# A round of its own for T1, its low parts on VectorE, a later bias add and a first pair worked two chunks at a time

## The chip, the cores and the metric

The kernel runs on one core of a Trainium2 chip. A core has TensorE (PE, matrix products into PSUM), ScalarE (ACT), VectorE (DVE) and GpSimd (POOL) for elementwise work, and SyncE (SP), which here only issues transfers; transfers are also issued from POOL's queue, and could be from ACT's. Each engine works its own queue in order, and engines wait for each other by semaphores. The metric is the device time of one execution in microseconds (us). The kernel before takes 494.98 us, the median of three runs (494.9 to 495.29).

## The reference, cut to what matters

The input x is 64 x 64 x 1024 float32 (B, C, T). Each batch element picks one of 16 matrices of 64 x 64; a gated low-rank feed-forward layer follows, and x is added back.

```python
y = einsum('bct,bcd->bdt', x, weights[condition])     # mixes the 64 channels of one b
logits = einsum('bsd,ed->bse', y, gate_w)             # 8 experts
w, sel = top_k(logits, 2); w = softmax(w)             # w_full: 8 weights, 6 of them zero
result = einsum('bsd,od->bso', y, base_w) + base_b
low = einsum('bsd,erd->ebsr', y, lora_A)              # 8 experts x rank 16
result += 2.0 * einsum('ebsr,eor,bse->bso', low, lora_B, w_full)
out = x + result
```

## The kernel before, in words

**Tiles.** The 4096 tokens (b, c) are 32 tiles of 128. For a tile i, the product z of x with all weights is formed first: lora_A (128 columns), gate (8) and base_w (1024), 1160 columns in all, in four chunks c = 0 to 3 of 344, 236, 344, 236 columns. The channel mixing comes afterwards, as a product of z with a 128 x 128 block matrix gathered for the tile (`bdr`), since it acts on tokens alone. Float32 accuracy comes from splitting each operand in a high part (a rounded copy in `fp32r`) and a low part (the rest), and from three matmuls high x high, high x low, low x high (`zstep`, line 306). A split is two steps: a copy on ACT that rounds (`copy`, line 202), and a subtraction on DVE (`sub`, line 199, two inputs in SBUF). The tiles are `xh`/`xl` for x, `wh`/`wl` for weights, `zh`/`zl` for z, `bdh`/`bdl` for the gathered matrix.

**Plain tiles and pairs.** The inner dimension (8 blocks of 128, index k) is cut in halves h of four blocks, the columns in halves n of 580. So the weights are four blocks B11, B12, B21, B22, each of 4 x 128 rows and 344 + 236 columns (s = 0, 1). The first four tiles (two pairs) are plain: z = x1 B1n + x2 B2n. The other 28 tiles go by pairs, by Strassen's method in its seven-product form: products p1 (B11), p2 (B21), q3 (B22), and p6, p7, q4, q5 with the weight sums T2, T3, T4, T1, where T1 = B11 + B12, T3 = B12 + B22, T2 = B11 + T3, T4 = B21 + T2. The order in the first such pair is p1, p2, q3, p6, p7, q4, q5 (`FIRST`), with `post` work of other chunks between them; p2 is accumulated onto p1 in p1's banks, once p1 has been copied out. B12 is used by plain tiles alone, and its place in SBUF (`BLOCK`) is that of T4: T4 is written over B12 when the plain tiles are done with it.

**Weights.** `load_w` brings a piece of two k blocks and one s (344 or 236 KB) into one of the staging buffers `st`; `split_w` splits it into `wh`/`wl`. For the plain tiles, 16 pieces go round staging buffers 0 to 3. For the sums, `sum_w(s, k)`, called four times, loads the four pieces of all blocks again into `st` 0 to 3, forms the four sums there (`plus`, line 259, two inputs in SBUF) and splits all four; the low part goes to DVE or POOL, as the planner finds. `st[4]` is the place into which the first Strassen pair copies p1 (`u`); its other partial results are in `st` 1 to 3.

**After a chunk.** `post` mixes: for c = 0, three matmuls (line 337) into bank a0 or a1, then `gate` (the router, on DVE and ACT, lines 363 to 378), a transpose of the scaled `low` on PE (`tr`, line 383) and its split `lth`/`ltl`; for c > 0, the low-rank products and the mixing together into bank o0 or o1. `finish` (line 344) adds the result to `xtok`, which holds the rows of x plus bias, and `store` writes a tile. For the first four tiles the bias is added on DVE or POOL (line 277) as soon as the rows have landed, ahead of all `finish` steps of the tile; for later ones a transfer with accumulation does it.

**What sets the order.** All steps are put in a list (`add`, with an engine, a cost, what they read and write), and `Program.run` plays a list schedule on those costs: a step's `due` time gives each earlier step the latest time at which it may start (`late`), and an idle engine takes the ready step with the smallest. `ORDER` gives the due times of the plain matmuls, `pr.horizon` those of other steps. Loads without inputs are held back until ten microseconds before their `late` (`early`). The instructions are issued in that order, so each engine's queue is fixed when the program is built, by estimated times. SP issues all loads of weights and x, POOL the gathers, the stores and the bias transfers.

**The start.** `ORDER` has chunk 0 of tiles 0 and 1 together, block by block, then chunk 1 of tile 0, chunk 1 of tile 1 and so on. 29 small matmuls on zeroed data run first (line 193).

Of the kernel before, what the change touches and what calls it, by code (L numbers as in the profile page):

```python
# [20 lines left out]
P = 128  # L21
# [35 lines left out]
class Program:  # L57
# [7 lines left out]
    def add(self, engine, cost, fn, reads=(), writes=(), due=None, first=False, lag=0.0, early=False):  # L65


        n = len(self.steps)
        engine, cost = (e if isinstance(e, (list, tuple)) else [e] for e in (engine, cost))
        deps = set()  # L70
        for b in list(reads) + list(writes):
            if b in self.writer:
                deps.add(self.writer[b])
        for b in writes:
            deps.update(self.readers.get(b, ()))
        for b in reads:
            self.readers.setdefault(b, []).append(n)
        for b in writes:
            self.writer[b], self.readers[b] = n, []
        deps.discard(n)  # L80
        self.steps.append(dict(eng=dict(zip(engine, cost)), fn=fn, deps=deps, first=first, lag=lag,
                               due=self.horizon if due is None else due,
                               early=early or (SP in engine and not reads)))

    def run(self):
        steps, n = self.steps, len(self.steps)
        succ = [[] for _ in steps]
        for i, s in enumerate(steps):
            for d in s["deps"]:
                succ[d].append(i)  # L90
        hop = lambda a, b: SAME[a] if a == b else HOP[a]
        late = [0.0] * n
        for i in reversed(range(n)):
            s = steps[i]
            c, e = min(s["eng"].values()), next(iter(s["eng"]))
            late[i] = min([s["due"] - c] + [late[j] - hop(e, next(iter(steps[j]["eng"]))) - s["lag"] - c
                                            for j in succ[i]])
        left = [len(s["deps"]) for s in steps]
        ready, end, by = [0.0] * n, [0.0] * n, [None] * n
        free = dict(START)  # L100
        cand = {e: set() for e in HOP}

        def offer(i):
            for e in steps[i]["eng"]:
                t = max([0.0] + [end[d] + hop(by[d], e) + steps[d]["lag"]
                                 for d in steps[i]["deps"]])
                if steps[i]["early"]:
                    t = max(t, late[i] - AHEAD)
                t += MARGIN if steps[i]["first"] else 0.0
                cand[e].add((i, t))  # L110

        for i in range(n):
            if not left[i]:
                offer(i)
        done = 0
        while done < n:
            best = None
            for e, c in cand.items():
                if c:
                    t = max(free[e], min(r for _, r in c))  # L120
                    if best is None or t < best[0]:
                        best = (t, e)
            t, e = best
            i, r = min(((i, r) for i, r in cand[e] if r <= t + 1e-9),
                       key=lambda q: (not steps[q[0]]["first"], late[q[0]], q[0]))
            for f in steps[i]["eng"]:
                cand[f] = {q for q in cand[f] if q[0] != i}
            end[i], by[i] = t + steps[i]["eng"][e], e
            free[e] = end[i]
            steps[i]["fn"](e)  # L130
            done += 1
            for j in succ[i]:
                left[j] -= 1
                if not left[j]:
                    offer(j)
        return max(end)
# [3 lines left out]
def cond_ffn_kernel(ctx, tc, xT, x, idx, cw, wall, bias, lb, out):  # L140
# [15 lines left out]
    def many(n, shape, dt, name):  # L156
# [6 lines left out]
    BLOCK = (("b11", "t4"), ("b21", "b22"))  # L163
# [3 lines left out]
    NXR, NXA, NZ = 6, 4, 3  # L167
    xr, xtok = many(NXR, [P, KH, P], F32, "xr"), many(3, [P, T], F32, "xtok")
    xh, xl = many(NXA, [P, KH, P], F32R, "xh"), many(NXA, [P, KH, P], F32R, "xl")
    st = many(5, [P, 2 * CS[0]], F32, "st")  # L170
# [6 lines left out]
        ("mx", 8), ("l2", 14), ("d", E), ("e", E), ("wf", E), ("s", 1), ("r", 1))}  # L177
# [7 lines left out]
    warm = sb.tile([P, 8], F32, name="warm")  # L185
    nc.vector.memset(warm, 0.0)
    nc.scalar.activation(warm, warm, AF.Exp)
# [34 lines left out]
    def split_x(r, pieces=1, hi=ACT, lo=DVE):  # L222

        j, n = take("xa", NXA), KH // pieces
        for k in range(0, KH, n):
# [4 lines left out]
                [("xr", r, b) for b in q] + [("xh", j, b) for b in q], [("xl", j, b) for b in q])  # L230
        return j

    def sum_x(o, a, b, f):
        keys = lambda r: [("xr", r, q) for q in range(KH)]
        add(DVE, tt_cost(P * KH), lambda e: nc.vector.tensor_tensor(xr[o], xr[a], xr[b], f),  # L235
            [k for r in (a, b) if r != o for k in keys(r)], keys(o))
# [4 lines left out]

    def load_w(j, h, n, s, k):
        add(SP, DMA * 8 * P * CS[s], lambda e: nc.sync.dma_start(piece(j, s), wall[h][n][s][:, k:k + 2, :]),
            writes=[("st", j, 0), ("st", j, 1)])

    def split_w(j, m, s, k, hi=ACT, lo=DVE):
# [4 lines left out]
        lo = lo if isinstance(lo, tuple) else (lo,)  # L251
        add(lo, [tt_cost(n, e) for e in lo], lambda e: sub(e, wl[m, s][:, a], piece(j, s), wh[m, s][:, a]),
            src + [("wh", m, s, b) for b in q], [("wl", m, s, b) for b in q])

    def sum_w(s, k):
        keys = lambda j: [("st", j, 0), ("st", j, 1)]

        def plus(o, a, b):
            add(DVE, tt_cost(2 * CS[s]), lambda e: nc.vector.tensor_tensor(piece(o, s), piece(a, s), piece(b, s), ALU.add),  # L259
                [q for j in (a, b) if j != o for q in keys(j)], keys(o))  # L260
        for j, (h, n) in enumerate(((0, 0), (0, 1), (1, 1), (1, 0))):
            load_w(j, h, n, s, k)
        plus(0, 0, 1)
        plus(1, 1, 2)
        plus(2, 2, 0)
        plus(3, 3, 2)
        for j, m in ((2, "t2"), (1, "t3"), (3, "t4"), (0, "t1")):
            split_w(j, m, s, k, lo=(DVE, POOL))

    def load_tok(i):  # L270
# [5 lines left out]
        if early:  # L276
            add((DVE, POOL), (1.22, tt_cost(T, POOL)), lambda e: eng[e].tensor_tensor(xtok[j], xtok[j], bias_bc, ALU.add),  # L277
                ["bias"], keys)
        else:
            add(POOL, 1.1, lambda e: nc.gpsimd.dma_start(xtok[j], bias.broadcast_to([P, T]), accum_op=ALU.add),  # L280
                writes=keys, lag=5.0)

    def load_cond(i):
# [7 lines left out]
        add(DVE, 0.25, lambda e: sub(e, bdl[j], bdr[j], bdh[j]), [("bdr", j), ("bdh", j)], [("bdl", j)])  # L291
# [63 lines left out]
    def gate(i, b):  # L355
# [9 lines left out]
        def op(o, a, f, eng=DVE, cost=0.17):  # L365
            add(eng, cost, lambda e: f(), [(b, i % 2) for b in a], [(b, i % 2) for b in o])

        ts, stt = nc.vector.tensor_scalar, nc.vector.scalar_tensor_tensor
        op(["mx"], ["low"], lambda: nc.vector.max(v["mx"], lg14))
        op(["d"], ["mx", "low"], lambda: ts(v["d"], lg, v["mx"][:, 6:7], None, ALU.subtract), cost=0.2)  # L370
        op(["e"], ["d"], lambda: nc.scalar.activation(v["e"], v["d"], AF.Exp), ACT, 0.2)
        op(["l2"], ["mx", "low"], lambda: nc.vector.match_replace(v["l2"], v["mx"], lg14, LOWEST), cost=0.25)
        op(["wf", "s"], ["l2", "e"], lambda: stt(v["wf"], v["l2"][:, :E], LOWEST, v["e"], ALU.is_equal, ALU.mult,  # L373
                                                 accum_out=v["s"]), cost=0.3)
# [3 lines left out]
            v["wf"].unsqueeze(2).broadcast_to([P, E, R]), ALU.mult, ALU.mult), cost=0.3)  # L378
# [32 lines left out]
    ORDER = [(i, 0, k) for k in range(KT) for i in range(2)]  # L411
    ORDER += [(i, c, k) for i, c in ((0, 1), (1, 1), (0, 2), (0, 3), (1, 2), (1, 3)) for k in range(KT)]
# [28 lines left out]

    def load_split_w(h, n, s, k, **engines):
        j = stage[0] % 4
        stage[0] += 1
# [7 lines left out]
    def first_loads():  # L452
        for h in range(2):
            for i in range(2):
                load_split_x(i, h, lo=DVE)
                load_split_w(h, 0, 0, 2 * i)
# [12 lines left out]
    for h in range(2):  # L469
        for k in range(0, KH, 2):  # L470
            load_split_w(h, 0, 1, k)
    load_cond(0)
    load_cond(1)
    for s in range(2):
        for h in range(2):
            for k in range(0, KH, 2):
# [8 lines left out]
                                                          ALU.subtract), lraw + ["lbh"], ["lbl"])  # L485
# [8 lines left out]
    zb = [f"z{take('z', 4)}" for _ in range(2)]  # L494
    for k in range(KT):
        for i in range(2):
            plain(i, 0, (k,), zb[i])
    for i in range(2):
        post(i, 0, split_z(CS[0], bank[zb[i]][:, :CS[0]], zb[i]))
    for i, c in ((0, 1), (1, 1), (0, 2), (0, 3), (1, 2), (1, 3)):  # L500
        b, n = f"z{take('z', 4)}", CS[c % 2]
        plain(i, c, range(KT), b)
        post(i, c, split_z(n, bank[b][:, :n], b))
        if c == 3:
            store(i, range(4))
    for q in range(1, NPLAIN):
        pr.horizon = ends[q] + LAG
        for i in (2 * q, 2 * q + 1):
# [4 lines left out]
            for c in range(4):  # L513
                b, n = f"z{take('z', 4)}", CS[c % 2]
                plain(i, c, range(KT), b)
                post(i, c, split_z(n, bank[b][:, :n], b))
            store(i, range(4))
    for s in range(2):
        for k in range(0, KH, 2):
            pr.horizon = ends[0] + (2 * s + k / 2 + 1) / 4 * (ends[NPLAIN - 1] - ends[0])  # L520
            sum_w(s, k)

# [41 lines left out]
    def pair(q):  # L564
        a, b = 2 * q, 2 * q + 1
        bx, by = (("z0", "z1"), ("z2", "z3"))[::1 if q % 2 else -1]
        u, v, w = 4 if q == NPLAIN else q % 2, 2, 3
# [3 lines left out]
        def combine(o, x, y, f, bs, reads=()):  # L571

            def then(s):
                at = {"o": part(o, s), "u": part(u, s), "v": part(v, s), "t": part(1, s), "z": z(bs, s)}
# [14 lines left out]
        if q == NPLAIN:  # L589

            t = 1
# [87 lines left out]
```

## Time and profile before

| | |
|---|---|
| median of three runs | 494.98 us (494.9 to 495.29) |
| the profiled execution's own time | 495.26 us |
| its span, first to last instruction | 493.5 us |
| PE busy | 480.2 us, 97% |
| DVE busy | 340.5 us, 69% |
| ACT busy | 173.2 us, 35% |
| POOL busy | 96.6 us, 20% |
| granted TensorE clock, mean | 0.993 |
| moved by transfers | 78.28 MB, 159 GB/s |
| loads of weights | 16 of 344 KB, 16 of 236 KB |

Times in the profile count from the start of the span. A line names the source line, the engine, the operation, what it writes and reads, and how often it ran. An arrow in "idle before" or in the list of waits names what ended the wait. The clock is a share of full speed. A busy time of matmuls is not throughput: they are pipelined, and the distance between starts tells their pace.

### The profile page before, as it was taken

The page shows a single profiled execution, that of the slowest core. Times are in us where ns is not written, and L with a number is a line of the kernel's source. Part 1 is how long each engine was busy: PE and PEld are TensorE (multiplying, and loading weights), DVE is VectorE, ACT ScalarE, POOL GpSimd, SP SyncE. Part 2 cuts the span into 40 slices and gives each one's busy share as a digit, 9 for nine tenths or more (in the row PEclk, how much of TensorE's full clock was granted, in tenths as well). Part 3 has the DMA queues.
Part 4 walks back from the last instruction along what each step waited for, and adds up shares of the span by engine and source line. Part 5 has one row for each costly group of instructions (what it writes and reads, how often), then busy time and mean ns, then how long its engine had stood idle before and what let it go on. Part 6 is the DMA issues. An engine that isn't in the chain of part 4 may idle for free.

```text
span 493.5 us, 9361 instructions
## 1 busy us (share of the span) xinstructions
PE 480.2 (97%) x3565; PEld 477.3 (97%) x3565; DVE 340.5 (69%) x930; ACT 173.2 (35%) x429; POOL 96.6 (20%) x110
## 2 busy tenths in 40 slices
PE   7999799899999999999999999999999999999996
PEld 6999799799999999999999999999999999999996
DVE  5768776885767666676667768666675686667664
ACT  6643324342332324233232433323232242323331
POOL 3015324411112030210203021030302103032010
PEclk8999999999999999999999999999999999999999
DMA  8793724942828275381835728192561727447162
GB/s 269 220 351 121 241 89 124 295 92 106 214 62 254 60 201 153 110 219 30 266 82 176 177 81 237 36 283 69 176 178 55 234 66 247 107 162 200 43 168 90
DMA packets 29325, 78.28 MB, mean 159 GB/s; under 512 B 3665, under 2 KB 7137, under 8 KB 29281
## 3 DMA queue, kind: packets, MB, share of 16 engines
q1 hardware_dynamic: 19872, 45.16, 27.7%
q0 software_dynamic: 9408, 32.53, 25.9%
q8 instruction: 28, 0.46, 0.4%
q14 instruction: 17, 0.13, 0.1%
HBM read 60.90 MB, written 16.78 MB: 157 GB/s over the span
## 4 chain that ended last, share of the span: by engine, by line
PE 85%; DMA 7%; DVE 4%; issue 1%; POOL 1%; ACT 1%; SPq 0%; DVEq 0%; POOLq 0%
PE ps_z L306 66%; PE ps_o L337 14%; DMA st<-in_w 6%; PE ps_a L337 5%; DVE st L259 2%; DMA xr<-in_xT 1%; POOL wl_t L199 1%; PE ps_a L383 1%; DVE xtok L344 1%; DVE wl_t L199 0%; DVE xl L199 0%; ACT wh_b L202 0%; DVE wf L373 0%; DVE zl L199 0%; DVE xtok L277 0%
## 5 line engine op out<-in xcount | busy, mean ns | idle before, releaser
L306 PE MATMUL ps_z<-wh_t,xh 128*128 128x344 f32 x480 | 143.7, 299 | 1.7 <-DVE st L576 1.3
L306 PE MATMUL ps_z<-wl_t,xh 128*128 128x344 f32 x480 | 142.6, 297 | 0.6 <-POOL wl_t L199 0.6
L306 PE MATMUL ps_z<-wh_t,xl 128*128 128x344 f32 x480 | 142.7, 297 | 0.0
L306 PE MATMUL ps_z<-wh_b,xh 128*128 128x344 f32 (+1 forms) x432 | 131.3, 304 | 2.0 <-ACT wh_b L202 1.4
L306 PE MATMUL ps_z<-wh_b,xl 128*128 128x344 f32 (+1 forms) x432 | 129.8, 300 | 0.4 <-DVE wl_b L199 0.4
L306 PE MATMUL ps_z<-wl_b,xh 128*128 128x344 f32 (+1 forms) x432 | 129.8, 300 | 0.2 <-DVE wl_b L199 0.2
L202 ACT CAST xh<-xr 128x512 fp32r<-128x512 f32 (+1 forms) x110 | 66.1, 605 | 83.6 <-PE ps_z L306 59.7
L199 DVE TENSOR_TENSOR xl<-xr,xh 128x512 fp32r<-128x512 f32 (+1 forms) x110 | 74.0, 677 | 28.0 <-ACT xh L202 26.2
L306 PEld LDWEIGHTS ps_z<-wh_t,xh 128*128 128x128 f32 x480 | 90.9, 189 | 2.3 <-DVE st L576 1.5
L306 PEld LDWEIGHTS ps_z<-wl_t,xh 128*128 128x128 f32 x480 | 91.0, 189 | 0.8 <-POOL wl_t L199 0.8
L306 PEld LDWEIGHTS ps_z<-wh_t,xl 128*128 128x128 f32 x480 | 90.8, 189 | 0.0
L306 PEld LDWEIGHTS ps_z<-wh_b,xh 128*128 128x128 f32 x432 | 83.0, 192 | 2.8 <-ACT wh_b L202 1.7
L306 PEld LDWEIGHTS ps_z<-wh_b,xl 128*128 128x128 f32 x432 | 82.8, 192 | 0.8 <-DVE wl_b L199 0.6
L306 PEld LDWEIGHTS ps_z<-wl_b,xh 128*128 128x128 f32 x432 | 82.9, 192 | 0.4 <-DVE wl_b L199 0.4
L344 DVE TENSOR_TENSOR xtok<-ps_o,xtok 128x344 f32<-128x344 f32 (+1 forms) x96 | 41.9, 438 | 33.5 <-PE ps_o L337 32.3
L202 ACT CAST zh<-st 128x344 fp32r<-128x344 f32 (+1 forms) x84 | 36.5, 436 | 72.6 <-PE ps_o L337 33.9
L351 POOL DMA_DIRECT2D out<-xtok x30 | 17.5, 585 | 209.8 <-DVE xtok L344 209.5
L576 DVE TENSOR_TENSOR st<-st,ps_z 128x344 f32<-128x344 f32 x84 | 38.0, 452 | 14.9 <-PE ps_z L306 14.9
L280 POOL DMA_DIRECT2D xtok<-in_bias x28 | 25.7, 917 | 109.0 <-DMA xtok<-in_x 107.7
L202 ACT CAST zh<-ps_z 128x344 fp32r<-128x344 f32 (+1 forms) x44 | 17.5, 401 | 72.7 <-PE ps_z L306 55.6
L235 DVE TENSOR_TENSOR xr<-xr,xr 128x512 f32<-128x512 f32 x56 | 38.5, 687 | 0.6
L199 DVE TENSOR_TENSOR zl<-st,zh 128x344 fp32r<-128x344 f32 (+1 forms) x84 | 37.9, 451 | 1.2 <-ACT zh L202 1.1
(71 smaller groups left out, 668.9 us busy)
## 6 DMA issues: line engine op xcount, KB each, us to landing
xtok<-in_x SPq DMA_DIRECT2D x32, 512.0 KB
xr<-in_xT SPq DMA_DIRECT2D x60, 256.0 KB
out<-xtok POOLq DMA_DIRECT2D x30, 512.0 KB, 5.3
xtok<-in_bias POOLq DMA_DIRECT2D x28, 512.0 KB, 5.3
st<-in_w SPq DMA_DIRECT2D x16, 344.0 KB
st<-in_w SPq DMA_DIRECT2D x16, 236.0 KB
xr<-in_xT SPq DMA_DIRECT2D x8, 128.0 KB
bdr<-in_cw,rows POOLq DMA_INDIRECT x32, 5.0
```

Of the source, the lines that this page charges most:

```text
L199: eng[e].tensor_tensor(o, a, b.bitcast(F32), ALU.subtract)
L202: (nc.scalar.copy if e == ACT else nc.vector.tensor_copy)(o, a)
L235: add(DVE, tt_cost(P * KH), lambda e: nc.vector.tensor_tensor(xr[o], xr[a], xr[b], f), [k for r in (a, b) if r != o for k in keys(r)], key ...
L259: add(DVE, tt_cost(2 * CS[s]), lambda e: nc.vector.tensor_tensor(piece(o, s), piece(a, s), piece(b, s), ALU.add), [q for j in (a, b) if j ...
L280: add(POOL, 1.1, lambda e: nc.gpsimd.dma_start(xtok[j], bias.broadcast_to([P, T]), accum_op=ALU.add), writes=keys, lag=5.0)
L306: nc.tensor.matmul(z, l[a][:, ka, :], w[m, s][:, ka, :], start=(start and q == 0), stop=(stop and q == 2), skip_group_check=True)
L337: nc.tensor.matmul(d, l, r, start=(start and m == 0), stop=(stop and m == len(mms) - 1), skip_group_check=True)
L344: add(DVE, 0.09 + 0.00104 * (s.stop - s.start), lambda e: nc.vector.tensor_tensor(xtok[j][:, o], bank[b][:, s], xtok[j][:, o], ALU.add), [ ...
L351: add(POOL, 1.0, lambda e: nc.gpsimd.dma_start(out[i * P:(i + 1) * P, o], xtok[j][:, o]), src, lag=2.0)
L383: add(PE, 0.107, lambda e: nc.tensor.matmul(tp, low[i % 2][:, :ER], ident, is_transpose=True, start=False, stop=False, skip_group_check=True),
L576: add(DVE, 0.09 + 0.00104 * CS[s], lambda e: nc.vector.tensor_tensor(at["o"], at[x], at[y], f), [bs[s]] + [("st", j, s) for j in reads if ...
```

## The change

1. **B12 and T1.** B12 takes the place of T1 in SBUF, no longer that of T4. `sum_w` forms and splits T3, T2 and T4 from the four loaded pieces. T1 has rounds of its own behind them (`sum_w1`, four calls), each of which loads B11's and B12's pieces anew, adds and splits them.
2. **Staging.** All weight pieces go round five staging buffers. The loads of weights are no longer held back. The first Strassen pair keeps its partial results in `st` 0, 4, 1, 2 (u, v, w, t), and its first products are in banks z0 and z1.
3. **DVE alone.** The low parts of T1 to T4 and the bias add of the plain tiles go to DVE only. The planner gets a flag (`port`) on DVE steps with two inputs in SBUF, such that two of these don't run at once in its plan.
4. **Bias.** For the first four tiles it is added behind the last `finish` of the tile, ahead of the store.
5. **The first pair.** Chunks 0 and 1 of tiles 0 and 1 are worked together, two k blocks at a time; the loads of weights for chunk 1 come in between. Then chunk 2 of both tiles and chunk 3 of both.
6. **The first piece of weights** is issued from ACT's queue, ahead of ACT's table load.
7. **The router.** The largest logit is negated on ACT and given to the exponential as its bias, in place of a subtraction on DVE, for all 32 tiles.

```diff
-    def add(..., lag=0.0, early=False):
+    def add(..., lag=0.0, early=None, port=False):
...
-                    t = max(free[e], min(r for _, r in c))
+                    t = max(free[e], min(max(r, port) if steps[i]["port"] else r for i, r in c))
...
+            if steps[i]["port"]:
+                port = end[i]
...
-    BLOCK = (("b11", "t4"), ("b21", "b22"))
+    BLOCK = (("b11", "t1"), ("b21", "b22"))
...
-    NXR, NXA, NZ = 6, 4, 3
+    NXR, NXA, NZ, NST = 6, 4, 3, 5
...
+    nc.scalar.dma_start(piece(0, 0), wall[0][0][0][:, 0:2, :])
+    begun = [True]
+    warm = sb.tile([P, 8], F32, name="warm")
+    nc.vector.memset(warm, 0.0)
+    nc.scalar.activation(warm, warm, AF.Exp)
...
     def load_w(j, h, n, s, k):
-        add(SP, DMA * 8 * P * CS[s], lambda e: nc.sync.dma_start(piece(j, s), wall[h][n][s][:, k:k + 2, :]),
-            writes=[("st", j, 0), ("st", j, 1)])
+        add(SP, DMA * 8 * P * CS[s], lambda e, begun=begun.pop() if begun else False: None if begun else
+            nc.sync.dma_start(piece(j, s), wall[h][n][s][:, k:k + 2, :]),
+            writes=[("st", j, 0), ("st", j, 1)], early=False)
...
     def sum_w(s, k):
...
-        plus(0, 0, 1)
-        plus(1, 1, 2)
-        plus(2, 2, 0)
-        plus(3, 3, 2)
-        for j, m in ((2, "t2"), (1, "t3"), (3, "t4"), (0, "t1")):
-            split_w(j, m, s, k, lo=(DVE, POOL))
+        b12, b22, b11, b21 = js = [next_stage() for _ in range(4)]
+        for j, (h, n) in zip(js, ((0, 1), (1, 1), (0, 0), (1, 0))):
             load_w(j, h, n, s, k)
+        for o, b, m in ((b12, b22, "t3"), (b11, b12, "t2"), (b21, b11, "t4")):
+            plus_w(o, o, b, s)
+            split_w(o, m, s, k)
+
+    def sum_w1(s, k, j):
+        for q in range(2):
+            load_w(j + q, 0, q, s, k)
+        plus_w(j, j, j + 1, s)
+        split_w(j, "t1", s, k)
...
-        if early:
-            add((DVE, POOL), (1.22, tt_cost(T, POOL)), lambda e: eng[e].tensor_tensor(xtok[j], xtok[j], bias_bc, ALU.add),
-                ["bias"], keys)
-        else:
+        if not early:
...
+    def late_bias(i):
+        j = i % 3
+        add(DVE, 1.22, lambda e: nc.vector.tensor_tensor(xtok[j], xtok[j], bias_bc, ALU.add), ["bias"],
+            [("xtok", j, c) for c in range(4)], port=True)
...
-        op(["d"], ["mx", "low"], lambda: ts(v["d"], lg, v["mx"][:, 6:7], None, ALU.subtract), cost=0.2)
-        op(["e"], ["d"], lambda: nc.scalar.activation(v["e"], v["d"], AF.Exp), ACT, 0.2)
+        op(["nm"], ["mx"], lambda: nc.scalar.mul(v["nm"], v["mx"][:, 6:7], -1.0), ACT, 0.2)
+        op(["e"], ["nm", "low"], lambda: nc.scalar.activation(v["e"], lg, AF.Exp, bias=v["nm"]), ACT, 0.2)
...
-    ORDER = [(i, 0, k) for k in range(KT) for i in range(2)]
-    ORDER += [(i, c, k) for i, c in ((0, 1), (1, 1), (0, 2), (0, 3), (1, 2), (1, 3)) for k in range(KT)]
+    ORDER = [(i, c, k) for h in range(0, KT, 2) for c in range(2) for i in range(2) for k in (h, h + 1)]
+    ORDER += [(i, c, k) for c in (2, 3) for i in range(2) for k in range(KT)]
...
                 load_split_x(i, h, lo=DVE)
-                load_split_w(h, 0, 0, 2 * i)
+                for s in range(2):
+                    load_split_w(h, 0, s, 2 * i)
...
+            pr.horizon += 8.0
+            late_bias(i)
             store(i, range(4))
+            pr.horizon -= 8.0
     for s in range(2):
         for k in range(0, KH, 2):
             pr.horizon = ends[0] + (2 * s + k / 2 + 1) / 4 * (ends[NPLAIN - 1] - ends[0])
             sum_w(s, k)
+    for s in range(2):
+        for k in range(0, KH, 2):
+            sum_w1(s, k, 1 + k)
...
-        bx, by = (("z0", "z1"), ("z2", "z3"))[::1 if q % 2 else -1]
-        u, v, w = 4 if q == NPLAIN else q % 2, 2, 3
+        bx, by = (("z0", "z1"), ("z2", "z3"))[::1 if q % 2 or q == NPLAIN else -1]
+        u, v, w, t = (0, 4, 1, 2) if q == NPLAIN else (q % 2, 2, 3, 4)
```

## The prediction

> **What bounds the kernel now.** I read the page first, for who is busy and when.
>
> ```profile
> PE 480.2 (97%) x3565; PEld 477.3 (97%) x3565; DVE 340.5 (69%) x930; ACT 173.2 (35%) x429; POOL 96.6 (20%) x110
> ...
> PE   7999799899999999999999999999999999999996
> ```
>
> PE is the bound; only slices 1, 5 and 8 (12.3 us each) and the last show gaps. From 100 to 480 us every stretch I asked for shows PE busy throughout: no edit can gain there, one can only lose. So the first 100 us decide. PE's list of waits, whole execution:
>
> ```profile
> PE ps_a L383 <- DVE low L376: 3.1, 1, 3.1
> PE ps_z L306 <- ACT wh_b L202: 1.4, 1, 1.4
> PE ps_z L306 <- DVE st L576: 1.3, 1, 1.3
> ...
> PE ps_z L306 <- POOL wl_t L199: 0.6, 1, 0.6
> ...
> PE ps_z L306 <- DVE zl L199: 0.4, 1, 0.4
> ```
>
> L383 is the transpose of tile 2's `low`. DVE's timeline shows what made `low` late:
>
> ```profile
> 53.13 0.88 DVE L259 TENSOR_TENSOR st<-st,st 128x688 f32<-128x688 f32 x1 [2.32 <-DMA st<-in_w]
> 53.92 0.17 DVE L369 MAX8 mx<-low 128x8 f32<-128x14 f32 x1
> ...
> 56.09 1.38 DVE L373 SCALAR_TENSOR_TENSOR wf<-l,e 128x8 f32<-128x8 f32 x1
> ...
> 57.60 1.21 DVE L277 TENSOR_TENSOR xtok<-xtok,bias_bc 128x1024 f32<-128x1024 f32 x1
> ...
> 59.15 0.34 DVE L376 SCALAR_TENSOR_TENSOR low<-low,r,wf 128x128 f32<-128x128 f32 x1
> ```
>
> The router stands behind a weight sum that waits 2.32 us for its piece; `wf` takes 1.38 us where its mean after 100 us is 0.158, because POOL's subtraction runs from 55.80 to 57.46; then the bias add stands ahead of `low`. And what made the piece late is in the chain:
>
> ```profile
> 45.99 2.26 POOL wl_t L199
> ...
> 48.27 4.76 DMA st<-in_w
> ...
> 71.38 2.39 POOL wl_t L199
> ...
> 73.78 2.89 DMA st<-in_w
> ```
>
> A staging buffer comes free when POOL's slow subtraction ends; only then is the next load issued. The one at 71.38 had waited for PE to finish with B12: T4 goes over it, so the next round's loads wait behind (SP waits 15.1 us). That round then crowds DVE at 88 to 95 us, where the last three waits of the list are. The start, on PE's timeline:
>
> ```profile
> 5.88 0.42 PE L306 MATMUL ps_z<-wh_b,xl 128*128 128x344 f32 x1
> 7.73 0.42 PE L306 MATMUL ps_z<-wh_b,xh 128*128 128x344 f32 x1 [1.43 <-ACT wh_b L202]
> ...
> 9.13 0.49 PE L306 MATMUL ps_z<-wh_b,xh 128*128 128x344 f32 x1
> ```
>
> Dense work begins at about 8.7, with starts 0.287 us apart until 11.7 and 0.157 after.
>
> **The Trainium skill.** "SBUF — State Buffer", Who interferes with whom: a DVE instruction with two SBUF inputs and a GpSimd one that reads SBUF exclude each other, and the loser blocks for the whole instruction. The trace agrees: 1.38 for 0.16, and a 688-wide L259 of 2.15 for 0.87 while POOL subtracts. "TensorE: Matmul & The Clock Gate", What's actually happening: the clock is halved by default and freed after about 3.4 us of activity. The trace agrees: 0.287 for 0.157 after the 3.07 us gap, for 2.8 us. "DMA: Bandwidth & Descriptors", Queues, rings and completion order: each DMA engine goes round between queues that have work. No run here shows a load from ACT's queue.
>
> **Parts 1 to 3, stalls.** The L383 stall is 3.07 us of idle time plus the slow clock: ten matmuls from 60.17 at 0.287 - 0.157 = 0.13 each, 1.3; together 4.4. The three of 90 to 95 are 0.37 + 0.56 + 1.31 = 2.24. Removed for good: POOL's ten subtractions (six of 1.90, four of 1.21 us) and their blocks on DVE, by excess over the ordinary duration 1.28 (L259 at 41.75), 0.78 (bdl, 47.33), 1.22 (wf), 1.00 (xl, 91.34): 4.3. Added to DVE: 6 x 0.79 + 4 x 0.56 = 7.0 (distance between starts in the same queue, 53.13 to 53.92 and 89.35 to 89.91), and one bias add, 1.1. T2 to T4 no longer touch B12, so their second half can run some 15 us sooner; T1 has till q5, after 97 us.
> New transfers: four pieces of 344 and four of 236 KB, 2.3 MB, and eight issues of 0.33 to 0.43 on SP. Hidden in 63 to 72 us, where the DMA share is 0.09; at 250 GB/s uncovered they would be 9 us. T1's loads stand in SP's queue behind buffers that PE frees late, with x loads behind them; before, all four x loads of that pair were out at 58, so I take 0 here, up to 1. The `port` flag is on DVE steps alone, which follow each other anyway: 0.
>
> **A new wait.** p1 is now copied into `st[0]`, which is in the staging ring; before it was `st[4]`, which no load used. p2 adds onto p1's bank, so it waits for that copy, and that for the last T2-T4 round to release buffer 0. Everything later on PE stands behind p2. DVE's load up to there:
>
> ```profile
> 30.00:80.10 50.10, 47.03 (x343) 46.52 (x342) 36.04 (x72) 17.31 (x39) 17.32 (x12) 0.97 0.52 179
> ```
>
> Of DVE's 36.04, blocks are 3.3, weight sums 8 x 0.79 + 0.56 = 6.9, low parts 2.1, bias adds 3.4; 20.4 remain. All of T2 to T4 is 12 sums and 12 subtractions, half wide: 12 x 0.79 + 12 x 0.56 = 16.2; with bias of tiles 0 and 1, 2.2: 38.8. p2 began at 81.33; earlier by start and first stall (2.4 + 4.4) that is 74.5, and the stretch from 27.6 to there is 46.9. Slack 8.1, against 14.1 of DVE idle before. With nine or ten of these left p2 is 1 to 2 late. I take 2.0 there and 0.8 for other waits of a plan with a fuller DVE: 2.8. Ends: 0, and 9 (the rival below).
>
> **Part 4.** The bias add leaves the way of `low` (counted) and is 1.1 us ahead of a store nobody waits for soon: 0. If DVE has no idle left behind it, zl waits 1.1.
>
> **Parts 5 and 6, the start.** By 11.70 PE has begun 15 wide matmuls, 15 x 0.157 = 2.4 us of full-pace work. Two k blocks now bring 352 + 242 + 2 x 131 = 856 thousand bytes, 2.5 us at the 350 GB/s of 7 to 12 us, for 12 x 0.157 + 12 x 0.111 = 3.2 us of matmuls; DVE needs 0.79 + 0.56 + 2 x 0.34 = 2.0 of it, ACT 1.8. So once begun PE doesn't starve, and tile 1's x is no longer behind a second piece of weights in ACT's queue (the 1.43 wait). If the first piece still lands at 3.82, PE is dense from 5.88: 11.70 - 5.88 + 0.3 = 6.1 us of work, gain 3.7. If ACT's queue shares the engines with SP's, its 352 thousand bytes end with 704 moved, 1.2 us later at 275 GB/s: dense from 7.05, gain 2.6. Each loses 1.3 if the clock drops as before: 3.7, 2.4, 2.6, 1.3. I take 2.4. A loss would need PE to begin 2.4 us later than all that; nothing speaks for it. Chunk 2 then begins at about 19; its weights were split by 18 to 22 before, with one buffer fewer: 0.
>
> **Part 7.** 32 DVE steps of 0.23 go, 32 on ACT of some 0.21 (as L371) come: 6.7 us on an ACT that is 35% busy. Behind it on ACT stands the exponential, which waited for DVE before. Ends -0.1 and +0.3; I take 0.
>
> **Sum.** Against the execution's own 493.5: -2.4 - 4.4 - 2.24 + 2.8 = -6.2, span 487.3. The profiled execution took 1.76 more than its span, and the median of the runs is 0.28 below it: 488.7.
>
> **Rivals.** *The stall comes back.* A router again stands behind a sum that waits for its piece, since DVE's queue is fixed by estimates and loads still take 2.5 to 4.8 us. For: L259 waits for transfers 9.0 us in 30 to 95 and there are now half as many loads again. Against: five buffers, freed by DVE in 0.8 where POOL took up to 2.4. One whole such stall (4.4) in place of my 2.8: 490.3; with another microsecond of waits 491.5. *All goes well.* No new wait, warm clock: 494.98 - 3.7 - 4.4 - 2.24 = 484.6. *The start does nothing*, because ACT or SP order its pieces badly: 488.7 + 2.4 = 491.1. *Slower: buffer 0 holds p2.* DVE keeps its 14.1 us of waits where 8.1 fit, and T1's first half (2 sums and 2 subtractions of 0.79) goes ahead: p2 is 6.0 + 3.2 = 9.2 late and finds the slow clock, 1.3 more. 494.98 - 9.0 + 10.5 = 496.5. It decides from a wait of 7.7. Against: DVE waits that come from having nothing else ready shrink when there is more to do; from 63 to 72 transfers idle. *It doesn't do what it says*: if rounds still crowded DVE at 88 to 95, only 2.24 is lost of the gain, within the forecast's range.
>
> **How the numbers follow.** Forecast 0.48 (486.5 to 490), stall back 0.18, start without gain 0.10, all well 0.11, slower 0.13. A measurement of this kernel tells 0.2% (1 us) from no change. The slower case is slower; at the top of the middle cases 0.03 fall within 0.2%, one in a hundred beyond: faster 0.83, same 0.03, slower 0.14. Range 484.8 to 493: below lies half of "all well", above the slower case.
>
> **What would show it.** Right: no POOL arithmetic after 10 us; no `wf` above 0.2; 40 loads of weights; PE dense from 6 to 7 us; L383 without a wait; no PE waits on `wl_t`; T2-T4's last sum ahead of p2. Wrong: PE waiting on ACT's `st` copy or idle ahead of p2 for more than 3 us; a clock of 0.5 anywhere after 12 us; PE begun later than 7.5; or any gap between 100 and 480.

## The result, and the profile after

The changed kernel takes 493.85 us (median of 20 runs, 491.79 to 496.61), the kernel before on the same chip 496.4 us (20 runs, 494.3 to 500.54). The ratio is 0.995, with a 95% interval of 0.9931 to 0.9969: faster by 0.5%, where 1.3% was forecast. Against the forecast's 6.3 us the gain is about 2.5. The kernel before took 1.4 us more in these runs than the 494.98 that the forecast started from; set against 494.98 the ratio gives 492.4.

The profiled execution of the changed kernel took 495.71 us (span 493.9), that of before 495.26 (493.5). The first lies near the slow end of its runs, the second near the fast end of its own, so what follows shows the loss at its large size.

The page of the changed kernel: busy time by engine, then PE and the granted clock in 40 slices of 12.3 us.

```profile
PE 480.5 (97%) x3565; PEld 478.6 (97%) x3565; DVE 342.4 (69%) x909; ACT 183.8 (37%) x461; POOL 85.0 (17%) x99
...
PE   8999968999999999999999999999999999999996
...
PEclk9999997999999999999999999999999999999999
```

POOL has lost 11.6 us and DVE has hardly gained (340.5 before). The gaps of slices 5 and 8 have become one deep place, slices 6 and 7 (62 to 86 us), and in the second of these the clock is down as well. PE's list of waits, whole execution (total, times, longest):

```profile
PE ps_z L322 <- DVE zl L199: 5.1, 2, 4.8
PE ps_z L322 <- ACT xh L202: 1.2, 1, 1.2
PE ps_o L193 <- DVE warm L246: 1.1, 1, 1.1
PE ps_a L399 <- DVE low L392: 1.0, 1, 1.0
PE ps_o L353 <- DVE ltl L199: 0.9, 1, 0.9
```

The router's stall of 3.07 us (L383, now L399) is down to 1.01, and the waits at 90 to 95 us to 0.25. A wait of 4.83 us has come in their place. PE's timeline has it at p1, the first product of the first Strassen pair (start, duration, what; idle before and its releaser in brackets):

```profile
75.94 0.66 PE L322 MATMUL ps_z<-wh_b,xh 128*128 128x344 f32 x1 [4.83 <-DVE zl L199]
76.39 0.49 PE L322 MATMUL ps_z<-wl_b,xh 128*128 128x344 f32 x1
```

p1 goes into bank z0. Tile 3's first chunk still lies there, although PE was done with it at 63.7 us. It leaves with `zh`, a copy on ACT, and then `zl`, a subtraction on DVE. From here to 80.41 us 15 wide matmuls begin 0.287 us apart in place of 0.157, and the four narrow ones up to 81.24 0.21 in place of 0.11: 2.4 us more. DVE's timeline ahead of it, then ACT's:

```profile
61.60 0.17 DVE L385 MAX8 mx<-low 128x8 f32<-128x14 f32 x1
...
64.53 0.88 DVE L265 TENSOR_TENSOR st<-st,st 128x688 f32<-128x688 f32 x1 [1.98 <-DMA st<-in_w]
65.32 0.15 DVE L391 RECIPROCAL r<-s 128x1 f32<-128x1 f32 x1
...
65.58 0.35 DVE L392 SCALAR_TENSOR_TENSOR low<-low,r,wf 128x128 f32<-128x128 f32 x1
...
71.40 0.65 DVE L265 TENSOR_TENSOR st<-st,st 128x472 f32<-128x472 f32 x1 [1.71 <-issue]
...
74.25 0.65 DVE L265 TENSOR_TENSOR st<-st,st 128x472 f32<-128x472 f32 x1 [1.60 <-DMA st<-in_w]
...
75.38 0.51 DVE L199 TENSOR_TENSOR zl<-ps_z,zh 128x344 fp32r<-128x344 f32 x1
```

```profile
72.08 0.59 ACT L202 CAST wh_t<-st 128x472 fp32r<-128x472 f32 x1 [4.40 <-DVE st L265]
72.58 0.44 ACT L202 CAST zh<-ps_z 128x344 fp32r<-128x344 f32 x1
```

All L265 shown are sums of T1. They wait for pieces of B11 and B12 (the releaser of the second is not in the records), and the reciprocal, `low` and `zl` stand behind them in the queue. ACT is held in the same way: its cast of T1's third sum waits for that sum, and `zh` stands behind the cast. Why the pieces come late is in the chain of work that ended last:

```profile
66.72 0.80 DVE wl_t L199
67.52 0.01 issue
67.53 6.62 DMA st<-in_w x2
```

T1's four rounds share two pairs of staging buffers. The first loads go out when the last rounds of T2 to T4 free these (59.99 us), the later ones when the split of the round before last has freed its pair, and the next sum then waits for the landing, 4.45 and 6.62 us in this chain. The planner counts with 1.3 us for a piece of 344 KB (`DMA`, 270 GB/s) and one more for the hop from SP; the page's medians from issue to landing are 4.8 us for such a piece and 3.9 for one of 236 KB. So its plan has sums ready that on the chip still wait.

The start: the first piece of weights, now from ACT's queue, is cast at 4.45 us (3.82 before), the first matmul is at 5.57, and from 6.63 PE is dense. By 11.70 it has begun 17 wide and 12 narrow matmuls, 4.0 us at the full pace, where before it had begun 15 wide ones, 2.4: 1.65 ahead (before rounding).

### The profile page after: what moved, and what is told of

It is laid out like the page before. It is cut to its first block, busy times and chain, and to the rows that moved or that the text cites. A ratio compares the mean times of both kernels' runs of the same rounds, so it can differ in the third digit from the quotient of the medians.

```text
span 493.9 us, 9323 instructions
## 1 busy us (share of the span) xinstructions
PE 480.5 (97%) x3565; PEld 478.6 (97%) x3565; DVE 342.4 (69%) x909; ACT 183.8 (37%) x461; POOL 85.0 (17%) x99
## 4 chain that ended last, share of the span: by engine, by line
PE 91%; DMA 4%; DVE 3%; issue 1%; ACT 0%; DVEq 0%
PE ps_z L322 71%; PE ps_o L353 14%; PE ps_a L353 5%; DMA st<-in_w 4%; DVE st L265 1%; DVE wl_t L199 1%; PE ps_a L399 1%; DVE xtok L296 0%; DVE xl L199 0%; DVE zl L199 0%; DVE xtok L360 0%; ACT wh_b L202 0%; ACT xh L202 0%; DVE bdl L199 0%; DVE r L391 0%
## 5 line engine op out<-in xcount | busy, mean ns | idle before, releaser
L322 PE MATMUL ps_z<-wh_t,xh 128*128 128x344 f32 (+1 forms) x480 | 143.0, 298 | 0.2 <-DVE zl L199 0.2
L322 PE MATMUL ps_z<-wh_t,xl 128*128 128x344 f32 (+1 forms) x480 | 142.7, 297 | 0.0
L322 PE MATMUL ps_z<-wl_t,xh 128*128 128x344 f32 (+1 forms) x480 | 142.5, 297 | 0.0
L322 PE MATMUL ps_z<-wh_b,xh 128*128 128x236 f32 (+1 forms) x432 | 132.8, 308 | 6.1 <-DVE zl L199 4.8
L322 PE MATMUL ps_z<-wh_b,xl 128*128 128x236 f32 (+1 forms) x432 | 130.0, 301 | 0.0
L322 PE MATMUL ps_z<-wl_b,xh 128*128 128x236 f32 (+1 forms) x432 | 130.0, 301 | 0.0
L302 POOL DMA_INDIRECT bdr<-in_cw,rows x32 | 39.0, 1219 | 24.3 <-DVE bdl L199 15.2
L199 DVE TENSOR_TENSOR zl<-ps_z,zh 128x344 fp32r<-128x344 f32 (+1 forms) x44 | 19.9, 456 | 30.9 <-ACT zh L202 30.9
```

The costliest lines, as they stand in the source:

```text
L199: eng[e].tensor_tensor(o, a, b.bitcast(F32), ALU.subtract)
L302: add(POOL, 1.04, lambda e: nc.gpsimd.indirect_dma_start(out=bdr[j], out_offset=None, in_=cw, in_offset=bass.IndirectOffsetOnAxis(ap=rows[ ...
L322: nc.tensor.matmul(z, l[a][:, ka, :], w[m, s][:, ka, :], start=(start and q == 0), stop=(stop and q == 2), skip_group_check=True)
```

## The experiments

Every run was compared with the kernel before on the same chip. Runs e1 to e4 share one chip and 15 runs of before (median 496.09), e5 to e8 another set (496.62), e9 to e12 a third (496.91).

| run | what | median us | ratio, 95% interval |
|---|---|---|---|
| (after) | the change | 493.85 | 0.995 [0.9931, 0.9969] |
| e1 | after, all weight sums due later | 487.44 | 0.9825 [0.979, 0.9859] |
| e2 | after, low parts of T1 to T4 on DVE or POOL | 490.57 | 0.9881 [0.9847, 0.9914] |
| e3 | before, with the new start alone | 499.61 | 1.0065 [1.0038, 1.0093] |
| e4 | after, first piece on SP | 492.11 | one run |
| e5 | before, all weight sums due later | 498.6 | 1.0056 [1.0038, 1.0074] |
| e6 | after, T1 alone due later | 486.76 | 0.9812 [0.9772, 0.9852] |
| e7 | after, T2 to T4 alone due later | 494.2 | 0.9949 [0.9933, 0.9965] |
| e8 | e1 with the first piece on SP | 487.05 | 0.9815 [0.9784, 0.9846] |
| e9 | after, T1's loads left out | 488.28 | 0.9833 [0.9793, 0.9872] |
| e10 | e6 with the start of before | 487.44 | 0.982 [0.979, 0.985] |
| e11 | e6 with the early bias add | 486.66 | 0.9797 [0.9766, 0.9828] |
| e12 | e6 with the first piece on SP | 486.32 | 0.9801 [0.9771, 0.9831] |

**e1, e2: the order, the load on DVE, or the transfers.** `sum_w` gives its steps due times at the quarters of the second plain pair; the router and the evictions of tiles 2 and 3 are due at that pair's end plus `LAG` (16). So wherever both are ready, a weight sum goes first. `sum_w1` sets no due time: it has what the loop before it left in `pr.horizon`, the pair's end. e1 changes one line in the loop of `sum_w`, and T1 inherits it:

```diff
-            pr.horizon = ends[0] + (2 * s + k / 2 + 1) / 4 * (ends[NPLAIN - 1] - ends[0])
+            pr.horizon = ends[NPLAIN - 1] + LAG
             sum_w(s, k)
```

> The changed kernel with one edit: the steps of T2 to T4's sums get the same due time as the other steps (end of the plain tiles plus LAG) in place of quarters of the second plain pair. Theory A (due times: the sums, due by the end of the plain tiles, stand ahead of tile 2's mixing and router on DVE, so the zh buffers and with them bank z0 come free late): PE's wait ahead of p1 falls from 4.8 to under 1 us, the slow clock at 76 to 81 us is gone, time 484.5 to 488, some 7 us below the changed kernel. Theory B (DVE's load: with POOL's ten subtractions DVE has too much to do before p1, in whatever order): the wait only moves, 4 us or more of PE waits with their slow clock stay between 50 and 95 us, time within 2 us of the changed kernel's 493.9. Theory C (transfers: the pieces land late): the sums' waits for pieces, 5.0 us in 27 to 97 us, stay or grow, and PE waits 3 us or more behind them.

e2 gives POOL a share of the low parts again:

```diff
-            split_w(o, m, s, k)
+            split_w(o, m, s, k, lo=(DVE, POOL))
...
-        split_w(j, "t1", s, k)
+        split_w(j, "t1", s, k, lo=(DVE, POOL))
```

> The changed kernel with one part undone: the low parts of T1 to T4 go to DVE or POOL, as the planner finds. Theory A: it helps in part; DVE is freed of up to 7 us, but single DVE instructions of 1 to 2 us blocked by POOL come back; p1's wait 0 to 2 us, 487 to 491. Theory B: the wait goes wholly, as little as 485 to 488, the best of these runs. Theory C: no gain, 492 to 495.

With the due times alone, 487.44 us: p1 waits for nothing, and after the start PE's only waits are 0.4 (`ltl`) and 0.2 us. DVE does the same work (340.2 us busy) and the same 40 loads of weights run. So neither the amount of work on DVE nor that of the transfers makes the changed kernel's stall by itself; another order of the same steps removes it. e2 gains half of e1's 6.4 us. Its p1 doesn't wait either: in its order tile 3's `zl` (70.66 us) stands ahead of T1's two narrow sums (72.60), and DVE waits only 1.4 us for pieces (5.0 in the changed kernel). Waits of PE of 0.9 and 0.8 us at the router and the mixing, and of 1.7 at an output sum, whose `xtok` rows were late, remain.

**e3, e4: the start.** e3 is the kernel before with parts 5 and 6; e4 is the changed kernel without part 6's queue:

```diff
-    nc.scalar.dma_start(piece(0, 0), wall[0][0][0][:, 0:2, :])
-    begun = [True]
+    begun = []
```

> The kernel before with the start alone: first pair two chunks at a time, first piece of weights from ACT's queue. All theories: by 11.7 us PE has begun 1.6 us more of full-pace work than before, as in the changed kernel; with the later stalls of the kernel before (4.4 and 2.2 us) unchanged the time is 1.6 below the kernel before; if these stalls depend on how early PE arrives, it is up to 3 us above or 6 below that.

> The changed kernel with the first piece of weights issued from SP again, ahead of its other loads. If the two queues share the DMA engines: the piece is cast at 3.8 us, not at 4.45, PE's first matmul is at 5.0, not at 5.57. If it landed late for another reason: 4.4 and 5.5 again. The rest of the kernel, and p1's wait of 4.8 us, stay as they are.

e3 is slower than before by 0.65% (3.2 us), more than its expectation allowed, although PE is 1.2 us of matmuls ahead at 11.7: the router's stall has grown from 3.07 to 5.0 us. What the start gives is taken back where DVE is late. In e4 the first piece is cast at 3.53 us in place of 4.45, and PE has begun 5.2 us of matmuls at 11.7, in place of 4.0. This agrees with what the prediction took from the Trainium skill ("DMA: Bandwidth & Descriptors", Queues, rings and completion order): with a second queue at work the first piece gets a share of the engines, and here that costs it 0.9 us. Eight traces with this piece in ACT's queue have the cast at 4.45 to 4.75, and the three with SP's (e4, e8, e12) at 3.52 to 3.79. Part of the 5.2 is the clock: e8 has the same start, but at half pace up to 9.7 us, and has begun only 4.5. Against the expectation p1's wait did not stay: it is 2.58 us in e4. One execution doesn't tell whether the start did this or the landing of the pieces.

**e5: the due times on the kernel before.** The same line as in e1, in the kernel before.

> The kernel before with one edit alone: its sums of weights get the due times of the router's steps (the end of the second plain pair plus 16), nothing else changed. Theory A (what held the router of tile 2 in the kernel before, too, was that the sums' early due times put them ahead of it on VectorE, not the amount of work or the copies of biases and low parts on GpSimd): the wait of 3.07 us at L383 and the three waits of 90 to 95 us fall below 1 us in sum, ratio 0.984 to 0.990. Theory B (the change's other parts, less work on GpSimd and the spared 80 loads' share, are needed for the gain that e1_due has): the L383 wait stays above 2 us, ratio 0.995 to 1.002.

It is slower, 1.0056, which neither expectation had. The router's stall has gone (no wait at L383), and PE waits 4.60 us at p1 and 2.65 at 93.5 instead. DVE is busy for all of 60 to 75 us, but in long instructions; the timeline of POOL and DVE ahead of p1:

```profile
73.12 2.78 POOL L277 TENSOR_TENSOR xtok<-xtok,bias_bc 128x1024 f32<-128x1024 f32 x1
...
73.63 2.30 DVE L373 SCALAR_TENSOR_TENSOR wf<-l,e 128x8 f32<-128x8 f32 x1
75.86 0.08 DVE L373 DVE_READ_ACCUMULATOR wf<-l,e 128x1 f32 x1
75.86 0.50 DVE L199 TENSOR_TENSOR zl<-ps_z,zh 128x344 fp32r<-128x344 f32 x1
```

`wf` is 0.16 us of work; it ends with POOL's bias add, and `zl` stands behind it. POOL is busy for 8.35 of the 15 us, with subtractions and this add, and other instructions of DVE are drawn out while it works: a wide L259 to 2.38 us from 0.87, an `xr` to 2.12 from 0.68. So the due times alone don't give the gain of e1: in the kernel before they only put the blocked instructions in front of another eviction. The trace points to part 3, which takes this work from POOL. That part 3 is what was needed no run shows by itself, since e5 lacks the other parts too, and e2, which gives POOL the subtractions again, still gains.

**e6, e7: which sums.** e6 adds one line ahead of T1's loop; e7 does the opposite half.

```diff
+    pr.horizon = ends[NPLAIN - 1] + LAG
     for s in range(2):
         for k in range(0, KH, 2):
             sum_w1(s, k, 1 + k)
```

> The changed kernel, with T1's four sums and splits alone due at the second plain pair's end plus 16; the sums of T2 to T4 keep their early due times. If T1's rounds ahead of the router and of the eviction of z0 (the additions at L265 between 64 and 75 us) are what costs the 4.8 us at p1: that wait falls below 1 us, ratio 0.982 to 0.987, as e1_due has. If the early sums of T2 to T4 push tile 2's mixing and router back before that: the wait of p1 stays above 2 us and the ratio is 0.990 to 0.996.

> The changed kernel with the other half of e1_due: the sums of T2 to T4 are due at the second plain pair's end plus 16, T1's rounds keep their due time at the pair's end, so that they stand ahead of the router. If the due times of T2 to T4 are the cause: no wait above 1.5 us after 60 us, ratio 0.982 to 0.987. If T1's are: p1's wait stays at 2 to 5 us or a wait for the router takes its place (L399, L353), ratio 0.989 to 0.996.

e6 has the whole gain of e1, e7 none of it: its p1 waits 5.78 us for `zl`. It is T1's rounds, not those of T2 to T4. p1 in e6:

```profile
70.01 0.42 PE L322 MATMUL ps_z<-wh_b,xh 128*128 128x344 f32 x1 [0.27 <-DVE zl L199]
```

The work by stretch (busy us and instructions on PE, PEld, DVE, ACT, POOL, then the clock, the transfers' share and GB/s), first the changed kernel,

```profile
65.00:70.00 5.00, 3.06 (x22) 2.64 (x22) 4.69 (x10) 1.70 (x3) 0.00 (x0) 1.00 0.65 200
70.00:75.00 5.00, 1.11 (x9) 0.94 (x7) 2.00 (x4) 1.00 (x3) 0.00 (x0) 0.95 0.88 293
```

then e6:

```profile
65.00:70.00 5.00, 4.33 (x35) 3.96 (x33) 5.00 (x10) 2.84 (x6) 0.00 (x0) 1.00 0.71 239
70.00:75.00 5.00, 4.99 (x35) 4.99 (x36) 4.26 (x12) 2.19 (x8) 0.00 (x0) 1.00 0.71 219
```

Just ahead of p1, where the changed kernel's PE starves, its DVE does 2.00 us of work in 5. In e6 DVE finds 4.26 to do. The T1 sums of e6 still wait for pieces (0.74 us at 74.27), but with the evictions ahead of them.

**e9: the wait or the place.** T1's eight loads are left out, and the rest of the program stays in its order, so the sums are made of what the buffers hold and T1's products are not those of the reference.

```diff
         for q in range(2):
+            begun.append(True)
             load_w(j + q, 0, q, s, k)
```

> The changed kernel without the eight loads of T1's rounds (the four sums and splits stay where they are in VectorE's and ScalarE's order, and work on what the buffers hold, so T1's products are not those of the reference; 2.3 MB of transfers less). If it is the waiting of those four sums for their transfers, in front of the router and of the eviction of z0, that costs the time (1.98, 1.71 and 1.60 us before three of them in the changed kernel): p1's wait falls below 1.5 us and the ratio is 0.983 to 0.988. If it is their place and their busy time (four sums and four splits, some 6 us of VectorE) alone: p1's wait stays at 3 us or more, ratio 0.991 to 0.996.

DVE's timeline with T1's two narrow sums in front of `zl` as before, and PE's line of p1:

```profile
68.72 0.64 DVE L265 TENSOR_TENSOR st<-st,st 128x472 f32<-128x472 f32 x1
...
69.89 0.64 DVE L265 TENSOR_TENSOR st<-st,st 128x472 f32<-128x472 f32 x1
...
71.01 0.51 DVE L199 TENSOR_TENSOR zl<-ps_z,zh 128x344 fp32r<-128x344 f32 x1
```

```profile
71.57 0.42 PE L323 MATMUL ps_z<-wh_b,xh 128*128 128x344 f32 x1 [1.33 <-DVE zl L199]
```

In the same place and with the same busy time, but without waiting, `zl` comes at 71.01 in place of 75.38, and p1 waits 1.33 us in place of 4.83, with the next matmuls at the full pace. So of the 4.83, some 3.5 and all of the slow clock's 2.4 come from the pieces' lateness; the place and the work by themselves cost 1.3. (With 2.3 MB less to move, other pieces may have come sooner as well; that part is not separated.)

**e8, e10, e11, e12: the other parts, with the stall gone.** e8 and e12 take part 6's queue away (as e4) in e1 and e6; e10 is e6 with before's start, e11 e6 with the bias of the plain tiles added early, but on DVE.

> The changed kernel with e1_due's due times and the first piece of weights issued by SyncE instead of ScalarE's queue. If the start is worth its 0.9 us earlier first cast, now that no stall behind it takes the gain back: 1 to 2 us below e1_due, ratio 0.978 to 0.982, first matmul at 4.6 to 5.0 us. If the start's gain is lost again in a later wait of VectorE: ratio as e1_due, 0.981 to 0.985.

> e6_t1_late's kernel with the start of the kernel before (one chunk of each tile at a time, first piece on SyncE, table of exponentials loaded first). With no stall behind it, this prices the start. If the new start is worth the 1.65 us of matmuls that the changed kernel has ahead at 11.7 us: 488 us, ratio 0.984 to 0.987. If the start's gain is lost in a later wait even without the stall: ratio 0.980 to 0.983, as e6_t1_late has.

> e6_t1_late's kernel with the biases of tiles 0 to 3 added ahead of their first chunk again, on VectorE (not on GpSimd as before). If the later place of these four additions is worth something: a wait of 1 us or more for VectorE's router or eviction between 27 and 75 us, ratio 0.984 to 0.988. If it is worth nothing once T1's sums are late: ratio 0.980 to 0.983.

> e6_t1_late's kernel with the first piece of weights issued by SyncE. If the 0.9 us earlier first piece is kept up to the end: 0.7 to 1.2 us below e6_t1_late, ratio 0.978 to 0.980. If VectorE's order between 60 and 75 us takes it back, as e8_due_sp's wait for ltl (0.9 us) did: ratio 0.980 to 0.983.

None differs from e6 by more than the intervals hold. By the two profiles the start keeps 1.0 us (span 484.7 in e6, 485.7 in e10; the medians differ by 0.7): e6 is 1.65 ahead at 11.7 us and meets waits of 0.41 and 0.27 us at 69 and 70 that e10 doesn't have. In e8 PE reaches tile 2's output sums 0.6 us earlier than in e1 (61.01 and 61.62), then waits 0.9 for `ltl` in place of 0.4, and from 68.5 on the two are level: DVE's order there doesn't move with PE. The lowest, e6, e11 and e12, stand at 0.980 to 0.981 and are not told apart, from each other or from e1, e8 and e10; set against the changed kernel, 0.9812 / 0.995 makes e6's one line worth 1.4%.

## Why the prediction went wrong, step by step

The direction was right, and the size was off by 3.8 us. The time lies above the range, by less than the 1.4 us by which the kernel before was slower in these runs; the gain itself is what fell short. Terms are set against the profiled execution's span, as the prediction's sum was:

| step | forecast us | measured us |
|---|---|---|
| start | -2.4 | -1.65 at 11.7 us |
| L383 stall with its slow clock | -4.4 | -3.4 (1.01 left, full clock) |
| three waits of 90 to 95 | -2.24 | -2.0 (0.25 left) |
| new waits | +2.8 | +8.2 (4.83 + 2.4 + 0.92) |
| sum | -6.2 | +1.1 |

The two profiled spans differ by +0.4, so 0.7 of this table is not placed.

- **The start** came out between the cases listed, near the 1.3 (queue shared, clock slow): the first piece is 0.63 us later than before, where the sharing case said 1.2, and the spacing is 0.287 us until about 9.5. That the clock was slow here was, as far as the runs show, chance: in e2 and e7, with the same start, matmuls ran at the full pace from the fourth on. Its worth at the end of the kernel is about 1 us by the profiles of e6 and e10, which is not clear of the noise.
- **Parts 1 to 3** removed what they were said to remove: no POOL arithmetic after 10 us, `wf` at 0.17, no PE wait on `wl_t`, 40 loads, nothing between 100 and 480. That DVE has room for the low parts was right too (e1, 340.2 us busy). e5 shows what POOL's blocks do to a plan with late due times, not that nothing else was needed.
- **The step that failed is "T1 has till q5, after 97 us".** That is when T1 is needed, not when the planner wants it. The code gives it the due time that the loop of T2 to T4 left behind, 16 ahead of the router's, and so its sums went in front of tile 2's `low` and tile 3's eviction. The loads were taken at "0 here, up to 1", as if a late T1 piece could hold up only T1. In DVE's queue it holds up all that stands behind: 1.98 + 1.71 + 1.60 us of idle DVE, and with them 4.83 us and the slow clock's 2.4 at p1, where 2.8 had been counted for all new waits. Nor did the loads find idle transfers: the DMA share was 0.65 and 0.88 from 65 to 75 us, where the prediction had read 0.09 for 63 to 72 in the kernel before. Both halves of the cause are shown: a later due time for T1 alone removes the wait (e6), and so in the main does leaving its loads out (e9).
- **The slack of 8.1 us** was a count of busy time, and the 2.8 was read off it for a wait ahead of p2 on `st[0]`. No such wait is in the list. The additions of T2 to T4 were done by 59.4 us; what was late was tile 3's eviction out of the bank that p1 takes, which the text did not consider. e1 and e6 have the same busy time and next to no waits, so a count of busy time could not have told the two apart.
- **The rivals.** "The stall comes back" had the mechanism, a router and what follows behind a sum that waits for its piece, but with one stall of 4.4 us at the old place. It came twice: small at `low`, large at z0. "Buffer 0 holds p2" had T1's first half going ahead on DVE, and the slow clock, but on the wrong buffer. A sharper reading of the due times would have given these two more than the 0.31 that they had.
- **Part 4, at 0,** agrees with e11 (0.9797, against 0.9812 without the undoing). Part 7 was not tried by itself; no wait in the profile points to it.

## What to carry to other kernels

Where a planner fixes in-order queues, read from the code which due time each new step gets, inherited ones too, and compare it with those of the steps whose delay stops the bound engine; when its result is needed is another number. Compare the plan's time for a load with the trace's, too: here some 2 us stood for 3.9 to 4.8. A plan with the measured times was not tried. An instruction that waits for a transfer charges its wait to everything behind it on its engine, so ask of each new load what stands behind its first reader. A gain at the start is kept only as far as the queues behind it leave room: here 1.65 us became about 1 by the profiles, and alone, in the kernel before, a loss of 3.2.

## What was not expected of the hardware

- **The half clock came in two lengths.** Read in steps of 0.1 us, the granted clock was at half for 3.41 us in before (from 59.46), and for 6.83 in the changed kernel (from 74.49, still in the gap of 4.83, to 81.32) and in e3, e4, e5 and e7. Start and end of the kernel aside, no trace has another length. The Trainium skill ("TensorE: Matmul & The Clock Gate", What's actually happening) puts the release at about 3.4 us of sustained activity; the traces show this length once or twice over, and twice costs 2.4 us of matmuls here, where the prediction counted 1.3 for once. So the prediction's price for a gap of 3.07 us was no price for every gap.
- **The length of one gap doesn't tell whether the clock falls.** It stayed full through gaps of 1.33 us in e9 and 2.65 in e5 (at 93.5). In e4 it fell at 69.80, ahead of the gap of 2.58 and behind two of only 1.17 and 0.93 us.
